# Dealing the rows of a mixture-of-experts layer to their places block by block, and turning each tile on VectorE

## The chip, the cores and the metric

The kernel runs on one core of one Trainium2 chip. The metric is device time in microseconds (us) for one execution. Three runs of the kernel before gave 1424.63, 1426.37 and 1427.61; their median, 1426.37, is the time that the change is measured against.

## What is computed

A GRU cell runs over 256 time steps for 8 sequences with state width 512. Its outputs, 2048 rows of 512 float32, go through a mixture of 8 experts, of which each row uses two, beside a shared expert that every row uses. The result is added to the input `x`.

```python
def cell(h, x):
    gi = x @ W_ih + b_ih
    gh = h @ W_hh + b_hh
    i_r, i_z, i_n = jnp.split(gi, 3, axis=-1)
    h_r, h_z, h_n = jnp.split(gh, 3, axis=-1)
    r = jax.nn.sigmoid(i_r + h_r)
    z = jax.nn.sigmoid(i_z + h_z)
    n = jnp.tanh(i_n + r * h_n)
    h_new = (1.0 - z) * n + z * h
    return (h_new, h_new)
...
probs = jax.nn.softmax(x @ w_gate, axis=-1)
topk_w, topk_ids = jax.lax.top_k(probs, 2)
topk_w = topk_w / jnp.sum(topk_w, axis=-1, keepdims=True)
combine = jnp.sum(topk_w[..., None] * jax.nn.one_hot(topk_ids, 8), axis=1)
act = _silu_and_mul(jnp.einsum('th,ehf->etf', x, w_gate_up))   # 512 -> 256
eo = jnp.einsum('eti,eih->eth', act, w_down)                   # 256 -> 512
routed = jnp.einsum('te,eth->th', combine, eo)
shared = _silu_and_mul(x @ w_sh_gate_up) @ w_sh_down           # 512 -> 1024 -> 512
return (routed + shared).reshape(orig_shape)
...
x = x + ffn(gru(cond_2048, x))
```

## The kernel before

**Stages.** Time is cut into 16 blocks of 16 steps, so a block holds 8 x 16 = 128 rows, one per partition. The profile shows four stages: loading and the first input projections (0 to 41.6 us), the recurrence (41.6 to 1154), a tail that finishes the last blocks' shared expert (1154 to 1204), and the tile stage, which does the routed experts (from 1204).

**The recurrence.** `step(n)` issues 32 small matmuls against the state and then a chain over VectorE (DVE) and ScalarE (ACT) to the new state. The schedule is written out by hand: between the matmuls of two steps TensorE (PE) gets a fixed amount of other work from `queue`: the input projections of the next block (`project`, line 331) and the shared expert of earlier blocks (line 785). In each step GpSimd (POOL) copies one column of `hn` to `last_hn` (line 523). That copy does no arithmetic that is needed; since POOL runs its instructions in order, it holds what stands behind it, such as the bias additions of `project` (line 425, `gi<-gi,bias`), until `hn` of that step is made.

**Routing.** After a block its rows are routed over the next block's steps: `choose`, `sum_logits`, `order_experts`, `weigh`, `count_places`, `give_places`. Then `enter` (line 637) writes for each row and each of its two experts one entry (row number and weight, 8 bytes) to a list `listed` in DRAM, at the row's place in its expert's part, by an indirect DMA of POOL; `send_rows` (lines 647 and 652) turns the block's states with one 128x512 transpose of DVE and stores the rows in token order to `rows` in DRAM. For block 0 `enter` runs eight times, once for each expert, in block 1. The last block's routing stands in the tail, in a hand-written list `routing` whose first numbers are places in the work of PE.

**The tail.** `lay_tiles` counts the rows of each expert, cuts each expert's part into tiles of 128 entries, reads the entries of all tiles back with one indirect DMA (line 697, `nT<-listed,at`), and makes `row` and `share`, the row numbers and weights of each tile, and `steer`, its expert. Meanwhile POOL loads the weights of two experts (line 170). SP, the engine that only issues DMAs, issues `send_rows`, then the stores of finished shared rows (`add_up`, line 824) and loads of `x` for the next ones (`load_again`, line 770).

**The tile stage.** 35 tiles are always run, with up to 4 more under a condition. `fetch_rows(i)` (line 836) gathers the tile's 128 rows from `rows` into `xr_i`, an indirect DMA of POOL; it is called two tiles ahead, and `xr` has three buffers. `before_` (lines 850 and 852) turns the rows: four 128x128 transposes on PE into PSUM, and one copy by ACT into `xrT`. The up matmuls (line 739), the activation (lines 726, 730, 731), the two transposes of the activation (line 750), the down matmuls (line 870) and the weighting by DVE into `y` (line 873) follow. At last an indirect DMA of POOL adds `y` to the rows of the output in DRAM (line 876). `y` has two buffers. `run_tile` lets three tiles overlap on PE:

```python
for work in [
    *(stages[0] if stages else []),     # before_ of tile i
    *ups[: NQ // 2],                    # first half of the up matmuls of tile i-1
    *(oldest[2] if oldest else []),     # the activation of tile i-2 is turned
    *ups[NQ // 2 :],
    *(oldest[3] if oldest else []),     # down matmuls of tile i-2
]:
```

**Waits between DMAs.** The framework tracks which DRAM tensor a DMA reads or writes, as a whole where the places come from an index. So each `enter` waits until the `enter` before it has landed, and each addition to the output waits for the one before it. The wait stands on the issuing engine, so everything behind it on POOL waits too.

Of the kernel before, what the change touches and what calls it, by code (L numbers as in the profile page):

```python
# [9 lines left out]
F32 = mybir.dt.float32  # L10
BF16 = mybir.dt.bfloat16
I32 = mybir.dt.int32
# [13 lines left out]
def kernel(  # L26
# [65 lines left out]
    NM = NTOK // P  # L92
    NW = NQ + NF
# [33 lines left out]
    def by_state(w):  # L127

        v = w.rearrange("(j q i) n -> j i q n", j=4, i=32)
        return [(slice(32 * j, 32 * j + 32), v[j]) for j in range(4)]  # L130

# [19 lines left out]
    h = state.tile([P, NQ, 32], F32, name="h")  # L151
# [34 lines left out]
    def load_up(e):  # L186
        for ps, src in by_state(w_gate_up[e]):
            load((we[ps, e, 0:NQ, :], src))
# [67 lines left out]
    first_place = counting("first_place", E, 0, NTOK, 0)  # L256
# [41 lines left out]
    listed = dram.tile([E * NM + 1, P, 2], F32, name="listed")  # L298
# [5 lines left out]
    load((listed[0 : E * NM], vacant), (listed[E * NM : E * NM + 1], vacant[0:1]))  # L304
# [229 lines left out]
    lg_of, rank_of, any_of, places_of, chosen, weight_of = {}, {}, {}, {}, {}, {}  # L534
    count = const.tile([P, E], BF16, name="count")
# [56 lines left out]
    def weigh_all(k):  # L592

        ch, w2 = chosen.pop(k), weight_of.pop(k)
        comb = said_0[:, :, 1]
        nc.vector.tensor_scalar(comb, ch[:, 0, :], w2[:, 0:1], None, ALU.mult)
        nc.vector.scalar_tensor_tensor(comb, ch[:, 1, :], w2[:, 1:2], comb, ALU.mult, ALU.add)
        nc.vector.tensor_scalar(
            said_0[:, :, 0], row_of.broadcast_to([P, E]), 0.0, None, ALU.add
        )  # L600
# [9 lines left out]
    def give_places(k):  # L610
        any_, ps = any_of.pop(k), places_of.pop(k)
        place = two.tile([P, E], F32, tag="place", name=f"place_{k}")
        nc.vector.tensor_tensor(place, ps, first_place, ALU.add)
        if k == 0:
            last = two.tile([P, E], F32, tag="last", name="last", bufs=1)
            nc.vector.tensor_scalar(last, any_, ahead, behind, ALU.mult, ALU.add)
            pl = two.tile([P, E], I32, tag="pl_0", name="pl_0", bufs=1)
            nc.vector.tensor_tensor(pl, place, last, ALU.add)
            nc.vector.tensor_copy(count, any_)
        else:  # L620
            ch, w2 = chosen.pop(k), weight_of.pop(k)
            nc.vector.tensor_tensor(ch, ch, place.unsqueeze(1).broadcast_to([P, 2, E]), ALU.mult)
            plf = two.tile([P, 2], F32, tag="plf", name=f"plf_{k}")
            nc.vector.tensor_reduce(plf, ch, AX.X, ALU.add)
            pl = two.tile([P, 2], I32, tag="pl", name=f"pl_{k}")
            nc.vector.tensor_copy(pl, plf)
            nc.vector.tensor_scalar(
                said[k % 2][:, :, 0], row_of.broadcast_to([P, 2]), float(k * TS), None, ALU.add
            )
            nc.vector.tensor_copy(said[k % 2][:, :, 1], w2)  # L630
            nc.vector.tensor_tensor(count, count, any_, ALU.add)
        places_of[k] = pl
# [11 lines left out]
    def send_rows(k):  # L644
# [6 lines left out]
        for j, c, ps in turns:  # L651
            nc.sync.dma_start(v[j, c, k * TS : (k + 1) * TS], hr[ps])

# [5 lines left out]
    def lay_tiles(part_no):  # L659

        if part_no == 0:
# [23 lines left out]
            spread = small([NT + 1], "spread", BF16)  # L685
            nc.vector.tensor_scalar(spread[:, 0:NT], ident[:, 0:NT], ex, None, ALU.mult)
            nc.vector.tensor_tensor(spread[:, NT:], ident[:, 0:1], cum[:, E - 1 : E], ALU.mult)
# [5 lines left out]
            nc.vector.scalar_tensor_tensor(no, ex, float(NM), no, ALU.mult, ALU.add)  # L693
            at = small([1], "at", I32)
            nc.vector.tensor_scalar(at, no, float(E * NM), None, ALU.min)
# [7 lines left out]
            laid.update(spread=spread, got=got)  # L703
        elif part_no == 1:
            ps = bank_of([P, NT + 1], "exp")[0]
            nc.tensor.matmul(ps, ones, laid["spread"], start=True, stop=True)
            steer = small([NT + 1], "steer", I32)
# [125 lines left out]
    def fetch_rows(i):  # L833
        if i < NT:
            xr_of[i] = xpool.tile([P, D], F32, tag="x", name=f"xr_{i}")
            nc.gpsimd.indirect_dma_start(
                out=xr_of[i],
                out_offset=None,
                in_=rows.rearrange("b t d -> (b t) d"),
                in_offset=bass.IndirectOffsetOnAxis(ap=laid["row"][:, i : i + 1], axis=0),  # L840
            )

    def tile_unit(i):
        box = {}

        def before_():
            ps = for_transposes([NQ, P], f"xrTp_{i}")
            xr = xr_of.pop(i)
            for q in range(NQ):
                nc.tensor.transpose(ps[:, q, :], xr[:, q * P : (q + 1) * P], ident)  # L850
            xrT = two.tile([P, NQ, P], F32, tag="xrT", name=f"xrT_{i}")
            nc.scalar.copy(xrT, ps)
# [104 lines left out]
    for k in range(NB):  # L957
# [7 lines left out]
        if k > 0:  # L965
# [5 lines left out]
            for t, (f, cost, busy) in enumerate(steps_):  # L971
                when(t + late, cost, busy, lambda f=f, k=k: f(k - 1))
            if k == 1:
                when(5, 0, 0.7, lambda k=k: weigh_all(k - 1))
# [48 lines left out]
    for e in (E - 4, E - 3):  # L1023
# [7 lines left out]
        (7 * MM, lambda k: lay_tiles(0)), (behind_them, lambda k: load_again(k - 1)),  # L1031
        (behind_them, load_again), (14 * MM, lambda k: lay_tiles(1)),
        (22 * MM, lambda k: lay_tiles(2)),
# [64 lines left out]
```

## Time and profile before

| | us |
|---|---|
| median of three runs | 1426.37 |
| the profiled execution, its own time | 1426.31 |
| its span (first to last instruction) | 1424.4 |
| loading and first projections | 0 to 41.6 |
| recurrence, block 0 and block 1 | 70.1 and 72.9 |
| recurrence, each of blocks 2 to 14 | 69.2 to 70.2 |
| tail | 1154 to 1204 |
| tile stage, first transpose to last instruction | 1204.0 to 1424.4 |
| PE busy in the tile stage up to 1412 | 204.0 of 208.0 |
| DVE, ACT and POOL busy in the same 208.0 | 56.7, 46.9 and 85.4 |

A line of a timeline reads: start and duration in us, engine, line of the kernel, operation, output<-inputs, shapes, count, and in brackets how long the engine stood idle before it and what ended that. "PEld" is PE loading weights, "SPq" a DMA issued by SP. The profiled execution lies 0.06 us from the median, and the span leaves 1.9 us of its time outside.

### The profile page before, as it was taken

To read this page: it belongs to the slowest core of one execution; us is meant where nothing else is said; L and a number is where in the kernel's file an instruction comes from. 1 tells how busy PE (TensorE), PEld (TensorE's weight loads), DVE (VectorE), ACT (ScalarE), POOL (GpSimd) and SP (SyncE) were. 2 spreads that over 40 slices of the span, in tenths; PEclk is the share of its full clock that TensorE was granted. 3 is DMA by queue.
4 is the path that set the end of the run, shared out by engine and by line. 5 is a ranking of instruction groups with operands and counts; after the bars stand their busy time and mean duration, and the time that the engine had idled before them with its cause. 6 is when DMAs were issued, how large, how long until landed. Compare 5 with 4: busy or idle time off the path is not lost.

```text
span 1424.4 us, 58403 instructions
## 1 busy us (share of the span) xinstructions
PE 1389.1 (98%) x24652; PEld 797.7 (56%) x24652; DVE 634.0 (45%) x2661; ACT 493.8 (35%) x2072; POOL 284.0 (20%) x525
## 2 busy tenths in 40 slices
PE   6999999999999999999999999999999999999995
PEld 2455557565666566656665666566656654444442
DVE  2345554455454545455544554554444541222221
ACT  0344343334333433343334343334343321222221
POOL 2233421212110201010101010101011221444442
PEclk9999999999999999999999999999999999999998
DMA  7233322122211111011111121111012444445543
GB/s 268 92 119 109 78 80 54 49 76 65 59 38 35 28 52 35 23 43 37 36 36 29 29 52 29 38 31 45 14 43 55 94 91 109 74 90 91 92 90 46
DMA packets 66885, 90.90 MB, mean 64 GB/s; under 512 B 12688, under 2 KB 44480, under 8 KB 66624
## 3 DMA queue, kind: packets, MB, share of 16 engines
q0 software_dynamic: 15104, 37.57, 12.5%
q1 hardware_dynamic: 50176, 48.60, 12.3%
q8 instruction: 195, 3.19, 1.0%
q10 hardware_dynamic: 1344, 1.00, 0.2%
q14 instruction: 66, 0.54, 0.1%
HBM read 56.80 MB, written 30.32 MB: 61 GB/s over the span
## 4 chain that ended last, share of the span: by engine, by line
PE 95%; DMA 2%; DVE 1%; ACT 1%; issue 1%; POOL 0%; SPq 0%; ACTq 0%; DVEq 0%; POOLq 0%
PE ps_rn L494 32%; PE gu_s L785 16%; PE ps_z L494 15%; PE gip L331 10%; PE gu_t L739 8%; PE po L331 8%; PE yp L870 4%; DMA gid_rz<-gi 1%; DMA x<-in_x_dram 0%; DMA we<-in_L_cond_b_hh_dram 0%; PE ps_x L850 0%; PE ps_rn L850 0%; PE ps_z L850 0%; DMA out_dram<-y,row 0%; PE lgp L542 0%
## 5 line engine op out<-in xcount | busy, mean ns | idle before, releaser
L494 PE MATMUL ps_rn<-we,hT 128*8 128x256 f32 x8192 | 492.9, 380 | 13.2 <-ACT ps_rn L466 8.9
L494 PEld LDWEIGHTS ps_rn<-we,hT 128*8 128x8 f32 x8192 | 224.3, 90 | 264.1 <-ACT ps_z L466 54.2
L494 PE MATMUL ps_z<-we,hT 128*8 128x128 f32 x8192 | 273.4, 273 | 0.0
L507 DVE STREAM_TRANSPOSE rT<-ps_rn 128x128 f32<-128x128 f32 x256 | 81.1, 317 | 431.1 <-PE ps_rn L494 431.1
L494 PEld LDWEIGHTS ps_z<-we,hT 128*8 128x8 f32 x8192 | 228.1, 90 | 51.3 <-issue 0.5
L511 ACT ACTIVATE rT<-rT 128x32 f32<-128x32 f32 x256 | 58.5, 229 | 529.5 <-DVE rT L507 522.1
L523 POOL COPY last_hn<-hn 128x1 f32<-128x1 f32 x256 | 46.8, 183 | 885.4 <-DVE hn L522 878.6
L785 PE MATMUL gu_s<-hc,wsu 128*32 128x256 f32 x3072 | 188.6, 379 | 0.8 <-ACT gi L424 0.8
L331 PE MATMUL gip<-we,xT 128*32 128x512 f32 (+3 forms) x1872 | 186.9, 522 | 1.6 <-DVE xT L224 1.6
L785 PEld LDWEIGHTS gu_s<-hc,wsu 128*32 128x32 f32 x3072 | 102.5, 110 | 58.9 <-issue 10.8
L739 PE MATMUL gu_t<-we,xrT 128*128 x280 | 131.7, 593 | 0.3 <-issue 0.3
L331 PE MATMUL po<-wsd,act_s 128*32 128x512 f32 (+3 forms) x1272 | 130.1, 509 | 0.0
L331 PEld LDWEIGHTS gip<-we,xT 128*32 128x32 f32 x1872 | 60.1, 111 | 71.3 <-issue 58.8
L507 DVE STREAM_TRANSPOSE zT<-ps_z 128x128 f32<-128x128 f32 x256 | 79.0, 309 | 0.4 <-PE ps_z L494 0.4
L528 ACT COPY hc<-hT 128x32 f32<-128x32 f32 x192 | 47.4, 247 | 91.3 <-DVE hT L525 90.0
L876 POOL DMA_INDIRECT out_dram<-y,row x35 | 55.5, 1585 | 112.9 <-DVE y L873 102.5
L730 DVE TENSOR_TENSOR act_t<-gu_t,act_t 128x256 f32<-128x256 f32 x35 | 14.9, 425 | 131.4 <-ACT act_t L726 131.4
L466 ACT COPY ps_rn<-seeds_n 128x128 f32<-128x128 f32 x256 | 69.0, 270 | 8.8 <-DMA seeds_n<-gid_n 0.6
L507 DVE STREAM_TRANSPOSE nT<-ps_rn 128x128 f32<-128x128 f32 x256 | 70.2, 274 | 0.0
L514 DVE TENSOR_TENSOR rT<-nT,rT 128x32 f32<-128x32 f32 x256 | 51.2, 200 | 41.3 <-ACT rT L511 40.7
L466 ACT COPY ps_rn<-seeds 128x128 f32<-128x128 f32 x256 | 68.9, 269 | 1.5 <-DVE rT L514 0.6
L739 PEld LDWEIGHTS gu_t<-we,xrT 128*128 128x128 f32 x280 | 47.9, 190 | 34.9 <-issue 34.7
(168 smaller groups left out, 1221.6 us busy)
## 6 DMA issues: line engine op xcount, KB each, us to landing
we<-in_L_ffn_w_gate_up_dram POOLq DMA_DIRECT2D x32, 256.0 KB, 3.8
seeds<-gid_rz SPq DMA_DIRECT2D x252, 32.0 KB
gid_rz<-gi SPq DMA_DIRECT2D x15, 512.0 KB
wsu<-_L_ffn_w_sh_gate_up_dram POOLq DMA_DIRECT2D x16, 256.0 KB, 3.8
rows<-hr SPq DMA_DIRECT2D x128, 32.0 KB
we<-in_L_ffn_w_down_dram POOLq DMA_DIRECT2D x16, 256.0 KB, 4.7
again<-in_x_dram SPq DMA_DIRECT2D x16, 256.0 KB
out_dram<-again SPq DMA_DIRECT2D x16, 256.0 KB
```

The costliest lines, as they stand in the source:

```text
L331: nc.tensor.matmul(ps[32 * c : 32 * c + 32], lhs(c), rhs, start=start, stop=stop, skip_group_check=True,)
L466: nc.scalar.copy(gate_of[g], src)
L494: nc.tensor.matmul(banks[g][32 * j : 32 * j + B, 0 : n_ * P].rearrange("b (a k i) -> b a k i", a=n_, k=NQ), hT[:, q, 0:B], whh_v[:, q, j, ...
L507: nc.vector.transpose(gT.rearrange("p a b -> p (a b)"), gate_of[g])
L511: nc.scalar.activation(r, r, AF.Sigmoid)
L514: nc.vector.tensor_tensor(r, nT[:, :, 0:B], r, ALU.mult)
L523: nc.gpsimd.tensor_copy(last_hn, hn[:, 0, 0:1])
L528: nc.scalar.copy(hc_of_block(k).rearrange("p g q (c t) -> p q g c t", t=TS)[:, :, :, :, t], new.rearrange("p q (g c) -> p q g c", c=2),)
L739: nc.tensor.matmul(box["ps"], lhs(q), w_up(q), start=(q == 0), stop=(q == NQ - 1))
L785: nc.tensor.matmul(box["ps"][32 * g : 32 * g + 32, two_i, :], wsu[c][:, q, two_i, fs], hc_of[m][:, :, q, :], start=(two_i == 0 and q == 0) ...
L870: nc.tensor.matmul(box["y"], lhs, rhs, start=(f == 0), stop=(f == NF - 1))
L876: nc.gpsimd.indirect_dma_start(out=out.rearrange("b t d -> (b t) d"), out_offset=bass.IndirectOffsetOnAxis(ap=laid["row"][:, i : i + 1], a ...
```

## The change

The rows no longer lie in token order for the tiles to gather. After `send_rows` a block's 128 rows are read back to SBUF in token order (`read_rows`, an SP DMA), and two indirect DMAs of POOL (`deal_rows`), one for each of a row's experts, scatter them to a second DRAM tensor, `dealt`, where each expert has 17 blocks of 128 places. In the tail eight more indirect DMAs write rows of zeros behind the last row of each expert, so that a tile's unused places hold zeros; a last block of `dealt` is all zeros from the start. A tile is then 128 rows that lie together. `fetch_rows` reads the tile's number from `steer` into a register of SP and issues four plain DMAs, each to 32 partitions: partition 32j+t gets elements 128j to 128j+127 of rows t, 32+t, 64+t and 96+t. One transpose of DVE in 32x32 blocks makes `xrT` of it; the four transposes of PE and the copy of ACT are gone. Since the features of a row now lie on the partitions in another order, an expert's up weights are loaded in plain blocks of 128 rows and not by quarters.

```diff
-    def by_state(w):
-
-        v = w.rearrange("(j q i) n -> j i q n", j=4, i=32)
-        return [(slice(32 * j, 32 * j + 32), v[j]) for j in range(4)]
...
-    h = state.tile([P, NQ, 32], F32, name="h")
+    h = we[:, 0, 3, 0:P].rearrange("p (q i) -> p q i", q=NQ)
...
     def load_up(e):
-        for ps, src in by_state(w_gate_up[e]):
-            load((we[ps, e, 0:NQ, :], src))
+        for q in range(NQ):
+            load((we[:, e, q, :], w_gate_up[e, q * P : (q + 1) * P, :]))
...
+    dealt = dram.tile([E * NR + 1, P, D], F32, name="dealt")
...
+    nothing = we[:, 1, 2]
+    nc.gpsimd.memset(nothing, 0.0)
...
+    load((dealt[E * NR], nothing))
...
+    def read_rows(k):
+
+        rows_of[k] = two.tile([P, D], F32, tag="y", name=f"rb_{k}")
+        nc.sync.dma_start(rows_of[k], rows[:, k * TS : (k + 1) * TS, :])
+
+    def deal(tile_, at):
+        nc.gpsimd.indirect_dma_start(
+            out=dealt.rearrange("r p d -> (r p) d"),
+            out_offset=bass.IndirectOffsetOnAxis(ap=at, axis=0),
+            in_=tile_,
+            in_offset=None,
+        )
+
+    def deal_rows(k, i):
+        deal(rows_of[k], rows_at[k][:, i : i + 1])
...
         elif part_no == 1:
-            ps = bank_of([P, NT + 1], "exp")[0]
+            ends = small([E], "ends")
+            nc.vector.scalar_tensor_tensor(
+                ends, laid["cnt"], part, first_place, ALU.add, ALU.add
+            )
+            ends_i = small([E], "ends_i", I32)
+            nc.vector.tensor_copy(ends_i, ends)
+            zeros = gi.rearrange("p j g n -> p (j g n)")[:, 0:D]
+            nc.gpsimd.memset(zeros, 0.0)
+            for e in range(E):
+                deal(zeros, ends_i[:, e : e + 1])
+        elif part_no == 2:
+            ps = bank_of([P, 2 * NT + 1], "exp")[0]
...
     def fetch_rows(i):
         if i < NT:
-            xr_of[i] = xpool.tile([P, D], F32, tag="x", name=f"xr_{i}")
-            nc.gpsimd.indirect_dma_start(
-                out=xr_of[i],
-                out_offset=None,
-                in_=rows.rearrange("b t d -> (b t) d"),
-                in_offset=bass.IndirectOffsetOnAxis(ap=laid["row"][:, i : i + 1], axis=0),
-            )
+            xr_of[i] = xpool.tile([P, NG, P], F32, tag="x", name=f"xr_{i}")
+            at = nc.values_load(
+                laid["steer"][0:1, NT + 1 + i : NT + 2 + i],
+                engines=(mybir.EngineType.SP,),
+                min_val=0,
+                max_val=E * NR,
+            )
+            src = dealt[bass.ds(at, 1)].rearrange("o (g t) (j m) -> j t (o g) m", g=NG, j=4)
+            for j in range(4):
+                nc.sync.dma_start(xr_of[i][32 * j : 32 * j + 32], src[j])
...
         def before_():
-            ps = for_transposes([NQ, P], f"xrTp_{i}")
-            xr = xr_of.pop(i)
-            for q in range(NQ):
-                nc.tensor.transpose(ps[:, q, :], xr[:, q * P : (q + 1) * P], ident)
             xrT = two.tile([P, NQ, P], F32, tag="xrT", name=f"xrT_{i}")
-            nc.scalar.copy(xrT, ps)
+            nc.vector.transpose(
+                xrT.rearrange("p q t -> p (q t)"),
+                xr_of.pop(i).rearrange("p g (q i) -> p q g i", q=NQ),
+            )
...
+            when(9, 0, 0, lambda k=k: read_rows(k - 1))
+            for i in range(2):
+                when(12 + i, 0, 0, lambda k=k, i=i: deal_rows(k - 1, i))
...
-        (7 * MM, lambda k: lay_tiles(0)), (behind_them, lambda k: load_again(k - 1)),
-        (behind_them, load_again), (14 * MM, lambda k: lay_tiles(1)),
-        (22 * MM, lambda k: lay_tiles(2)),
+        (7 * MM, lambda k: lay_tiles(0)), (8 * MM, lambda k: lay_tiles(1)), (9 * MM, read_rows),
+        (11 * MM, lambda k: deal_rows(k, 0)), (11 * MM, lambda k: deal_rows(k, 1)), (behind_them, lambda k: load_again(k - 1)),
+        (behind_them, load_again), (14 * MM, lambda k: lay_tiles(2)),
+        (22 * MM, lambda k: lay_tiles(3)),
         (22 * MM, lambda k: fetch_rows(0)), (22 * MM, lambda k: fetch_rows(1)),
```

In the built program of the changed kernel every one of the eight zero deals and of the two deals of the last block waits for the completion of the deal before it, and the first DMA of `fetch_rows(0)` waits for the last of them. On POOL the tail's order is: the two `enter`, two loads of weights, the read of the list, one load of weights, the zeros, the eight zero deals, three loads, the two deals of the last block, one load.

## The prediction

> **What bounds the kernel now.** I read the page's engine shares and chain first, then the tile stage's timeline, where the removed work stands, then POOL and PE in the tail, and last the end of the chain.
>
> ```profile
> PE 1389.1 (98%) x24652; PEld 797.7 (56%) x24652; DVE 634.0 (45%) x2661; ACT 493.8 (35%) x2072; POOL 284.0 (20%) x525
> ...
> PE 95%; DMA 2%; DVE 1%; ACT 1%; issue 1%; POOL 0%; SPq 0%; ACTq 0%; DVEq 0%; POOLq 0%
> ```
>
> PE is busy for 98% of the span and carries 95% of the chain that ends last, so an instruction taken from PE is worth its own time, until something else ends later. One tile, from the timeline of the tile stage:
>
> ```profile
> 1233.33 1.57 POOL L876 DMA_INDIRECT out_dram<-y,row  x1 [2.93 <-DVE y L873]
> ...
> 1237.90 0.60 PE L850 MATMUL ps_x<-ident,xr 128*128 128x128 f32 x4
> ...
> 1238.34 1.88 PE L739 MATMUL gu_t<-we,xrT 128*128 x4
> ...
> 1239.14 1.58 POOL L876 DMA_INDIRECT out_dram<-y,row  x1 [2.95 <-DVE y L873]
> ```
>
> A tile takes 5.81 us (1233.33 to 1239.14). The four transposes hold PE from 1237.90 to 1238.34, 0.44 us. POOL's additions wait for DVE here, that is for PE.
>
> POOL in the tail, and PE where the tail becomes the tile stage:
>
> ```profile
> 1163.44 1.04 POOL L637 DMA_INDIRECT listed<-said,pl  x1 [6.21 <-DVE count L631]
> 1166.85 1.01 POOL L637 DMA_INDIRECT listed<-said,pl  x1 [2.37 <-DMA listed<-said,pl]
> 1167.86 0.59 POOL L170 DMA_DIRECT2D we<-in_L_ffn_w_down_dram  x1
> 1168.43 0.60 POOL L170 DMA_DIRECT2D we<-in_L_ffn_w_gate_up_dram  x1
> 1172.23 1.02 POOL L697 DMA_INDIRECT nT<-listed,at  x1 [3.20 <-DMA listed<-said,pl]
> ...
> 1184.61 1.00 POOL L836 DMA_INDIRECT xr<-rows,row  x1 [8.55 <-DVE share L718]
> ```
>
> ```profile
> 1203.97 0.65 PE L850 MATMUL ps_x<-ident,xr 128*128 128x128 f32 x4
> ...
> 1205.35 3.67 PE L739 MATMUL gu_t<-we,xrT 128*128 x8 [0.28 <-issue]
> ```
>
> PE has shared work until 1203.97. The first gather leaves at 1184.61, so the tile stage's first rows have some 15 us of cover. An indirect DMA that waits for the one before it starts 3.41 us (1163.44 to 1166.85) to 5.38 us (1166.85 to 1172.23) after it.
>
> The end of the chain shows the same for the additions:
>
> ```profile
> 1407.30 4.65 DMA out_dram<-y,row
> ...
> 1412.70 1.55 POOL out_dram L876
> ```
>
> The addition issued at 1407.30 lands after 4.65, and the next starts at 1412.70: a link of 5.40 us, 4.65 to land and 0.75 for POOL to wake and issue.
>
> **The change, part by part.**
>
> *The tile stage.* Without the four transposes PE needs 5.81 - 0.44 = 5.37 us per tile. DVE's 128x512 transpose is priced by the one of `send_rows` (L647, 0.71 us). DVE has 56.7 us busy in 208.0 and takes 35 x 0.71 = 24.9 more; it is off the path, since the turn of tile i is wanted only one tile later. ACT loses its copies, PE waits for neither. POOL loses 35 gathers of 0.98 us. But the additions form a chain of their own:
>
> ```profile
> xr<-rows,row POOLq DMA_INDIRECT x35, 4.1
> out_dram<-y,row POOLq DMA_INDIRECT x35, 4.7
> ```
>
> These are the median times from issue to landing. With 4.7 + 0.75 a link is 5.45 us. Before, that was under PE's 5.81; it is over the new 5.37, so the additions, not PE, pace the new stage. Bounds: 5.37 (PE) and 5.73 (1379.31 to 1385.04, the one place in the stage where POOL waited for an addition). I take 5.45, the median. Before, the first up matmul stood at 1205.35 and the last addition at 1412.70: 207.35. After: 10.55 (1205.35 to the first addition at 1215.90) less one tile's 0.44, and 34 x 5.45 = 185.3: 195.4. **-11.9 us** (-14.7 with PE alone, -2.4 with 5.73).
>
> SP gets four plain DMAs and a register load per tile. Eight stores of 512-byte pieces took SP 5.55 us in `send_rows`, 0.69 each, so 2.8 per tile; the register load would have to cost over 2.6 before SP paces the stage. I take it as hidden, two tiles ahead; the cover gone, each tile would be late by the excess.
>
> A page of the Trainium skill prices the removed work otherwise: "VectorE: DVE Perf Modes", The three transpose paths, gives a 128x128 transpose 390 ns on TensorE, which would make an estimated 35 x 4 x 0.39 = 55 us of gain. Those are bfloat16 and single; in this trace four float32 ones, back to back, take 0.44 us, and the sum goes by that.
>
> *The tail.* This is new on the path. The read of the list ends on POOL at 1173.25; one load follows (0.56), then 128x512 zeros, which I estimate at 0.5 from the 0.20 of a 128x128 memset of POOL and 0.10 of a tiny one. So the first zero deal starts at 1174.4. Ten deals, each waiting for the one before, make nine links and a landing. No row shows a plain scatter of 2 KB rows. Below stands `enter`, the same write of 8-byte rows: 3.41. Above stands the addition, which reads as well: 5.40. Nearest is the gather, the same bytes in as many rows with no addition: 3.6 for the one at 1187.19, 4.1 in the median, plus 0.75: 4.35 to 4.85. I take 4.5, of which 3.75 to land: 1174.4 + 9 x 4.5 + 3.75 = 1218.6. The loads of weights lie in the same queue, one ahead of the first deal and three ahead of the ninth; the second `enter` of the tail, with loads in its way, took 2.0 more than the first, and I add 2.8 for both places (0 to 5): 1221.5.
>
> Then SP wakes (0.3), issues four DMAs (3 x 0.69 to the last), which land after 2.58 (the `seeds` load on the chain at 29.05): 1226.4. DVE turns the rows in 0.71, with its wake 0.8: the first up matmul stands at 1227.2, not 1205.35. **+21.9 us**, for which PE is idle from 1204. Bounds: 1213.5 (+8.1) with links of 3.41 and no loads in the way, 1238.4 (+33.1) with 5.40 and 5. Three things stand behind the waits: SP's last two stores, needed ten us later by the first addition; four loads of the sixth expert, not needed for half of the tile stage; the next `fetch_rows`, which follow in 3 us each while an up stage takes 3.44.
>
> The Trainium skill's "DMA: Bandwidth & Descriptors", Anatomy of one DMA, speaks against a chain of dependent writes in kind but prices it lower: about 2.0 us fixed plus bytes at 436 GB/s. By that a deal of 256 KB lands in an estimated 2.6 us, and with the same 0.75 the chain is ended some 11 us earlier and the change about even. The landings above are all over 2.6, so the rows decide.
>
> *The recurrence.* Each block gains an SP read and two deals on POOL at steps 12 and 13. SP's wait for `send_rows`, issued two or three steps earlier, is over by then, and the loads queued behind it (`seeds`) are wanted four steps later. POOL waits in the second deal for the first, less than two steps, and behind it stands only `last_hn`, wanted by the next `hn`. From block 2 on no bias addition stands near the deals in the built order: nothing. Block 1 differs, with eight `enter` and bias additions among them:
>
> ```profile
> 146.25 1.28 POOL L425 TENSOR_TENSOR gi<-gi,bias 128x512 f32<-128x512 f32 x1
> 146.27 1.32 DVE L515 TENSOR_TENSOR rT<-nT,rT 128x32 f32<-128x32 f32 x1
> ```
>
> POOL had waited for an `enter`, the bias addition slid into DVE's chain, and a 0.19 us operation of DVE took 1.32; that step took 6.24 us where its neighbours take 4.3. Block 1 is 3.5 over the others for this. Two deals more at its steps 12 and 13, just ahead of a bias addition, cost one such step more: **+2.0 us** (0 to 5).
>
> The rest is small: plain weight loads in place of quarters (256 KB each as before), a dozen tiny DVE operations, a memset of 0.5 us at the start.
>
> **Sum.** -11.9 + 21.9 + 2.0 = +12.0 on the profiled execution's 1426.31, 0.06 under the median: **1438.3 us**.
>
> **The rivals.**
>
> *The cover nearly holds* (faster). If a scattered write of 2 KB rows lands like `enter`'s, the tile stage starts at 1213.5, and with PE pacing it and no loss in block 1 the sum is 8.1 - 14.7 = -6.6: 1419.7. For it: the two `enter` at 1163.44. Against: an `enter` moves 1 KB, a deal 256 KB, and the gather, which moves as much, lands later. With my other terms kept, the links must fall under 3.3 for no change; with every other term at its best, under 4.05.
>
> *The tile stage gains nothing as well* (much slower). If the additions are slowed by the plain loads beside them to 5.73, or SP paces the stage at about that, it gains 2.4: 21.9 + 2.0 - 2.4 = +21.5, 1447.8. For it: DMA is busy 47% of that stage. Against: half of the indirect DMAs there are the gathers, which go.
>
> *It balances.* Links near 3.5: +2, 1428. That the deals don't wait, so that the change would do only what it removes, is excluded by the built program, where each of them waits for the last.
>
> **How the numbers follow.** Forecast 0.74, much slower 0.12, faster 0.08, balance 0.06. 0.2% is 2.9 us, about what a measurement of this kernel can tell. Only the third is under 1423.5, only the fourth within: faster 0.08, same 0.06, slower 0.86. The range leaves out most of the faster case and the far end of the slow one: 1426 to 1453.
>
> **What would show it.** Right: PE idle for over 15 us after 1204, ended by DVE's turn of `xr`; on POOL eight deals, 4 to 5 us apart, each waiting for a deal; additions 5.4 to 5.5 us apart, now waiting for a DMA. Wrong in size: links under 3.5 or over 5.4. Wrong in kind: the first `fetch_rows` before 1200, or tiles paced by SP.

## The result, and the profile after

The changed kernel takes 1431.94 us in the median (1424.12 to 1440.62, 22 runs), the kernel before beside it 1426.24 (1424.63 to 1429.48, 22 runs): a ratio of 1.0034, 95% interval 1.0023 to 1.0045, or +5.7 us where +12.0 was forecast. Measured twice more, on two chips, the ratio was 1.0073 (1.0056 to 1.0090) and 1.0075 (1.0059 to 1.0090), some +10.5 us. In the first measurement the changed kernel's 22 times lie 16.5 us apart and those of the kernel before 4.9; in the two others 6 times of the changed kernel lie 7 apart, 17 of the kernel before 7 to 8. That the ratio differs from one measurement to the next belongs to the explanation. The profiled execution took 1429.51, its span is 1427.7.

The page's engine line of the chain that ended last (shares of the span) gives PE 90% where it had 95%, and DMAs, issue and POOL the rest:

```profile
PE 90%; DMA 4%; issue 2%; DVE 1%; POOL 1%; ACT 1%; SPq 0%; POOLq 0%; ACTq 0%; DVEq 0%
```

The tail, from the timelines of POOL and PE (start, duration, engine and line, operation, idle time before it and what ended that):

```profile
1178.17 1.03 POOL L661 DMA_INDIRECT dealt<-gi,ends_i  x1 [0.28 <-POOL gi L731]
1184.08 0.98 POOL L661 DMA_INDIRECT dealt<-gi,ends_i  x1 [4.88 <-DMA dealt<-gi,ends_i]
...
1201.65 0.96 POOL L661 DMA_INDIRECT dealt<-gi,ends_i  x1 [2.02 <-DMA dealt<-gi,ends_i]
...
1212.84 0.99 POOL L661 DMA_INDIRECT dealt<-rb,pl  x1 [2.38 <-DMA dealt<-rb,pl]
```

```profile
1202.04 5.33 PE L331 MATMUL po<-wsd,act_s 128*32 128x512 f32 x48
...
1220.12 6.84 PE L769 MATMUL gu_t<-we,xrT 128*128 x12 [12.75 <-DMA xr<-dealt]
```

The ten deals stand in a row, each waiting for the one before, and PE stands idle for 12.75 us until the first rows have been fetched. That is the mechanism of the prediction, with shorter links: 2.98 us (1198.67 to 1201.65) for the shortest, 5.91 for the first, 34.67 for all nine. The chain that ended last shows what a short link is made of (start, duration, what):

```profile
1198.67 2.71 DMA dealt<-gi,ends_i
1201.38 0.27 issue
```

The deal lands after 2.71, and POOL starts the next one 0.27 later.

The additions, from the costliest groups (busy, mean ns of one, then POOL's idle time before them and what ended most of it) and from the DMA issues (the last number is the median from issue to landing):

```profile
L908 POOL DMA_INDIRECT out_dram<-y,row x35 | 54.3, 1552 | 151.0 <-DMA out_dram<-y,row 93.2
```

```profile
out_dram<-y,row POOLq DMA_INDIRECT x35, 4.7
```

POOL's waits ahead of an addition are now ended for the most part by the addition before (93.2 of 151.0 us), not by DVE. The 34 links take 186.5, 5.485 each.

Term by term, for two pairs of profiled executions, the second pair (runs e13 and e12 below) from one chip. Each difference is taken between the same two marks of the kernel before and after (last state: the last `last_hn`; then the first up matmul, the last addition's start, the end of the span):

| | forecast | first pair | second pair |
|---|---|---|---|
| up to the last state | +2.0 | 1153.91 to 1157.23: +3.3 | 1155.45 to 1153.68: -1.8 |
| last state to first up matmul | +21.9 | 51.44 to 62.89: +11.5 | 51.42 to 63.74: +12.3 |
| first up matmul to last addition | -11.9 | 207.35 to 198.06: -9.3 | 207.46 to 208.45: +1.0 |
| last addition to the end | 0 | 11.70 to 9.52: -2.2 | 11.87 to 9.73: -2.1 |
| span | +12.0 | +3.3 | +9.4 |

So the tail's term was nearly twice too large in both pairs, and the gain of the tile stage is there in one execution and gone in another. The second pair comes near the forecast because the two errors cancel, not because its terms were right.

### The profile page after: what moved, and what is told of

Same layout as the page of the kernel before. It is cut to its first block, busy times and chain, and to the rows that moved or that the text cites. A ratio compares the mean times of both kernels' runs of the same rounds, so it can differ in the third digit from the quotient of the medians.

```text
span 1427.7 us, 58770 instructions
## 1 busy us (share of the span) xinstructions
PE 1375.5 (96%) x24512; PEld 787.6 (55%) x24512; DVE 658.3 (46%) x2703; ACT 473.1 (33%) x2037; POOL 288.9 (20%) x533
## 3 DMA queue, kind: packets, MB, share of 16 engines
q8 instruction: 194, 3.18, 0.9%
## 4 chain that ended last, share of the span: by engine, by line
PE 90%; DMA 4%; issue 2%; DVE 1%; POOL 1%; ACT 1%; SPq 0%; POOLq 0%; ACTq 0%; DVEq 0%
PE ps_rn L494 32%; PE ps_z L494 15%; PE gu_s L815 14%; PE gip L331 10%; PE gu_t L769 9%; PE po L331 6%; PE yp L902 4%; DMA dealt<-gi,ends_i 1%; DMA out_dram<-y,row 1%; DMA gid_rz<-gi 1%; DMA x<-in_x_dram 0%; DMA listed<-said,pl 0%; DMA we<-in_L_cond_b_hh_dram 0%; DVE rT L514 0%; DMA seeds<-gid_rz 0%
## 5 line engine op out<-in xcount | busy, mean ns | idle before, releaser
L769 PE MATMUL gu_t<-we,xrT 128*128 x280 | 132.9, 598 | 12.8 <-DMA xr<-dealt 12.8
L769 PEld LDWEIGHTS gu_t<-we,xrT 128*128 128x128 f32 x280 | 51.1, 193 | 64.7 <-issue 57.0
L908 POOL DMA_INDIRECT out_dram<-y,row x35 | 54.3, 1552 | 151.0 <-DMA out_dram<-y,row 93.2
L522 DVE TENSOR_TENSOR hn<-hT,rT 128x32 f32<-128x32 f32 x256 | 49.3, 193 | 38.7 <-ACT rT L517 11.4
```

The source lines that it names most:

```text
L522: nc.vector.tensor_tensor(hn, hT[:, :, 0:B], nn, ALU.subtract)
L769: nc.tensor.matmul(box["ps"], lhs(q), w_up(q), start=(q == 0), stop=(q == NQ - 1))
L908: nc.gpsimd.indirect_dma_start(out=out.rearrange("b t d -> (b t) d"), out_offset=bass.IndirectOffsetOnAxis(ap=laid["row"][:, i : i + 1], a ...
```

## The experiments

The theory had two parts: the serial deals in the tail cost some 12 us of PE's idle time, and the tile stage without transposes is paced by the chain of additions, whose landing is not the same in every execution. The rivals: that the idle stretch comes from SP's plain fetches or from loads of weights; that bytes, not links, set the deals' length; that fetches or PE pace the stage. Where nothing else is said, an experiment is an edit of the changed kernel. Their readings, from the same marks (e5 is left out, see there; e3 and e13 are single executions):

| | last state to first up matmul | PE idle | us per tile (34 links) | ratio to before (95%) |
|---|---|---|---|---|
| before; again (e13) | 51.4; 51.4 | 0.3; 0.3 | 5.79; 5.79 | 1 |
| changed; again (e7, e12) | 62.9; 64.4, 63.7 | 12.8; 14.2, 13.6 | 5.49; 5.87, 5.77 | 1.0034; 1.0073, 1.0075 |
| e1, three zero deals | 54.2 | 3.2 | 5.81 | 1.0022 (1.0011 to 1.0033) |
| e5b, zeros in block 15 | 52.3 | 1.8 | 5.78 | 1.0006 (0.9995 to 1.0017) |
| e3, zeros twice | 85.9 | 35.7 | 5.51 | 1455.55 us, one run |
| e15, loads behind | 67.8 | 17.6 | 5.75 | 1.0065 (1.0044 to 1.0085) |
| e2, plain writes | 65.4 | 15.2 | 5.31 | 0.9986 (0.9974 to 0.9997) |
| e8, e5b with plain writes | 52.3 | 1.8 | 5.31 | 0.9892 (0.9877 to 0.9908) |
| e9, whole rows | 64.6 | 14.5 | 5.73 | 1.0077 (1.0056 to 1.0099) |
| e11, three fetches | 65.3 | 15.2 | 5.66 | 1.0055 (1.0042 to 1.0068) |
| e4, block 0's deals late | 64.8 | 14.7 | 5.75 | 1.0091 (1.0071 to 1.0110) |
| e14, zeros brought by SP | 52.2 | 1.8 | 5.89 | 1.0014 (1.0001 to 1.0027) |

**e1: fewer deals.**

```diff
-            for e in range(E):
-                deal(zeros, ends_i[:, e : e + 1])
+            deal(zeros[:, 0:D], near)          # 16 rows behind each expert's last
+            for i in range(2):                 # 128 x 4 rows, groups of four
+                nc.gpsimd.indirect_dma_start(
+                    out=dealt.rearrange("r (g s) d -> (r g) (s d)", s=4), ...
```

> The eight zero deals of the tail are replaced by three: one that writes 16 rows behind each expert's last, and two of 128 rows of 8 KB. Ten deals in a chain become five. Theory (the number of serial links sets the start of the tile stage, 3.85 a link): the wide deals land later than the narrow ones, about 6.5 a link, so the chain shortens by 9 x 3.85 - (2 x 3.85 + 2 x 6.5) = 14 at most; the idle stretch of PE of 12.75 shrinks to 0 to 3 and the time lies at 1415 to 1421, under the kernel before. Rival (bytes, not links: the two wide deals move 1 MB each against 256 KB, so the chain's 2.56 MB become 2.75 MB): the chain keeps its length within 2 us, and so does the time, 1430 to 1434.

The two wide deals made links of 6.47 and 8.47 (in the second, three loads of weights are issued behind that deal's landing), and the last of the five deals was issued 10 to 11 us sooner after the last state than the last of the ten. PE's idle stretch fell to 3.24, close to the 0 to 3 of the theory. The time did not follow: 1430.52, where the forecast was under the kernel before. The tile stage took 5.81 a tile, no less than before the change (5.79), so that nothing is left of its gain. What the edit is worth depends on the measurement of the changed kernel that it is held against: some 7 us by the ratios of 1.0073 and 1.0075, nothing clear of noise by 1.0034. It comes near the kernel before and no further.

**e5 and e5b: no zeros in the tail.** Both deal 256 rows of zeros for each expert in block 15 of the recurrence, behind the counts after block 14; the last block's rows then overwrite some of them.

```diff
+            if k == NB - 1:
+                for i, t in enumerate((9, 10, 11, 14, 15)):
+                    when(t, 0, 0, lambda i=i: deal_zeros(i))
...
-        (7 * MM, lambda k: lay_tiles(0)), (8 * MM, lambda k: lay_tiles(1)), (9 * MM, read_rows),
+        (7 * MM, lambda k: lay_tiles(0)), (9 * MM, read_rows),
```

> The zeros are written in block 15 of the recurrence, behind the counts that hold after block 14, by five deals (one of 128 rows of 2 KB, four of 128 rows of 8 KB, 256 rows for each expert); the tail keeps only the last block's two deals, and a POOL memset of 128x2048 is made at the start. Theory (the changed kernel loses its gain in the tail, because the chain of ten deals ends 12.75 us after PE has run out of shared work): the last deal lands some 30 us earlier, PE goes from the shared expert to the tile stage without an idle stretch, as before the change, and the tile stage and its end keep their -9.3 and -2.2: the span is 1427.7 - 12.8 - about 1.5 of low clock behind it = 1413 to 1416, ratio to the kernel before 0.991 to 0.995. Rival A (the idle stretch comes from the plain fetch by SP or from the wait of the register load, not from the deals): first up matmul still 10 us or more behind the end of the shared work, time about 1431. Rival B (the tile stage is slower as such once it starts early, since DMAs of weights lie beside it): idle stretch gone, but the stage takes 203 or more in place of 198, time 1420 or more.

In e5 I had put the source of zeros where the recurrence's weights `whh` lie. It ran 39 tiles in place of 35, 1451.4 us, and nothing rests on it. e5b keeps the zeros in the last expert's place, whose weights then load later:

> The zeros are written in block 15 by five deals as before, from space that is free then (the last expert's weights are loaded later for it); the tail keeps the last block's two deals. Two theories of what limits the changed kernel. Both say that PE's idle stretch goes (0 to 2 us) and that the first up matmul stands at about 1206. If the tile stage is paced by the additions at 5.6 to 5.8, it is no shorter than before the change, and the time is 1206 + 11.5 + 34 x 5.7 + 9.5 + 1.9 = 1423, ratio to the kernel before 0.995 to 0.999. If it is paced by PE or by a steady 5.485, the time is 1415, ratio 0.991. The rival that POOL's or SP's loads, not the zeros, hold the first fetch: first up matmul still at 1215 or later, time 1431 or more.

```profile
1207.22 5.33 PE L348 MATMUL po<-wsd,act_s 128*32 128x512 f32 x48
...
1214.36 5.39 PE L818 MATMUL gu_t<-we,xrT 128*128 x12 [1.81 <-issue]
```

The first up matmul follows the last shared matmuls after 1.81: the zero deals, and neither SP's fetches nor the loads, made the idle stretch. The recurrence ended 8 later here than in e12 (start 1.4, block 1 3.6 and block 15 3.0 longer), so the stage starts only 3 earlier; and it takes 5.78 a tile. The time is 1431.36: 10.6 under the changed kernel of the same call (1441.95), and no different from the kernel before, since the tile stage with its additions is no shorter than before the change.

**e2: additions become writes.**

```diff
-                    compute_op=ALU.add,
```

> A tile's result is written to the output's rows instead of being added to them (so the sums are left out); everything else is as in the changed kernel, and each write still waits for the one before. Theory (the additions pace the tile stage at 5.485 a tile, over PE's 5.37, since each lands after 4.7): a write without reading lands after 3.2 to 3.7, the link falls to about 4.3, POOL waits for DVE again, and PE paces the stage at 5.37: 34 x 0.115 = 3.9 us less, 1428, and the times scatter less. Rival (PE and its weight loads pace the stage at 5.485 and POOL's waits for the DMA are only what is left over): no change, 1430 to 1433.

The same lines of POOL's timeline, a tile apart:

```profile
1305.72 0.96 POOL L908 DMA_INDIRECT out_dram<-y,row  x1 [4.41 <-DVE y L905]
1311.09 0.96 POOL L908 DMA_INDIRECT out_dram<-y,row  x1 [4.41 <-DVE y L905]
```

POOL waits for DVE again, all steady tiles take 5.37 (PE's pace as forecast), the write lands after 3.0 in place of 4.7 to 4.9, and the 12 times lie 5.2 apart. The expected 1428 became 1425.62. So what the adding costs beyond a plain write stands between the changed tile stage and PE's pace.

**e8: both at once** (e5b and e2 together).

> Zeros in block 15 and, besides, a tile's result written in place of added (the sums are left out). Theory (two costs, each by itself: the deals in the tail cost some 12, the additions the difference from 5.37 a tile): first up matmul at about 1206, 5.37 a tile: 1206 + 12.3 + 34 x 5.31 + 11.7 + 1.9 = 1412, ratio 0.988 to 0.991. Rival (DMAs of weights or the fetches limit the stage once it starts early): over 5.45 a tile, 1416 or more.

1415.7 us, 14.6 under the kernel before (1430.28 beside it). Neither edit alone does this: e5b comes to 1.0006 of the kernel before, e2 to 0.9986, both together to 0.9892. In the profiled execution (1418.25, the slowest of the five) the first up matmul to the last write takes 190.8 where e13 has 207.5. Of these 16.7 the last link, 3.43 in place of PE's 5.37, is 1.9; the rest, 14.8, is what the prediction gave the stage with PE alone (-14.7). That the whole time also comes to -14.6 is partly chance: in the profile the recurrence ended 6.6 later than in e13.

**e7, e13 and e12: the same kernels again.**

> The changed kernel itself once more, beside the next ones. Theory (its tile stage is paced by additions whose landing differs from execution to execution, 4.7 to 5.0, since the runs with additions showed 5.485, 5.745 and 5.81 a tile and the one with plain writes 5.37): 5.6 to 5.8 a tile here, idle stretch of PE ahead of the first tile 12 to 15, median 1435 to 1441, and executions 10 or more apart. Rival (the slow tile stages of the two other kernels were due to their own edits): 5.45 to 5.5 a tile and a median of 1430 to 1434.

> The kernel before itself once more, for its profile beside the changed kernel's in one call. Theory (PE's 5.81 a tile hides the additions before the change): additions land after 4.7 to 5.0 as in the other runs, POOL's waits for them are few, and the tile stage keeps 5.81 a tile and some 207 from the first up matmul to the last addition. Rival (this chip or moment slows every tile stage): 5.85 or more a tile here too.

> The changed kernel beside the kernel before. Theory (the additions' landing is what differs between executions, and only the changed kernel feels it): over 5.5 a tile, first addition to last 187 to 200, idle stretch 12 to 15, 1433 to 1442, ratio 1.003 to 1.009. Rival (the first profile's 5.485 is the rule): 1431 to 1433, 5.45 to 5.5 a tile.

The kernel before kept 5.79 a tile, though its additions landed after 4.9 on that chip, as the changed kernel's did; the changed kernel took 5.87 and 5.77, where e7's expectation had 5.6 to 5.8. (The additions of the first profile landed after 4.7 in the median, those of e7 and e12 after 4.9.) The groups of e13 and of e12:

```profile
L876 POOL DMA_INDIRECT out_dram<-y,row x35 | 55.5, 1586 | 112.9 <-DVE y L873 105.4
```

```profile
L908 POOL DMA_INDIRECT out_dram<-y,row x35 | 54.3, 1552 | 161.3 <-DMA out_dram<-y,row 96.5
```

DVE's timeline in e12 shows how the additions take over:

```profile
1340.29 0.42 DVE L760 TENSOR_TENSOR act_t<-gu_t,act_t 128x256 f32<-128x256 f32 x1 [2.70 <-ACT act_t L756]
...
1341.92 0.75 DVE L905 TENSOR_SCALAR y<-yp,share 128x512 f32<-128x512 f32 x1 [0.75 <-DMA out_dram<-y,row]
...
1347.58 0.75 DVE L905 TENSOR_SCALAR y<-yp,share 128x512 f32<-128x512 f32 x1 [1.03 <-DMA out_dram<-y,row]
...
1351.04 0.42 DVE L760 TENSOR_TENSOR act_t<-gu_t,act_t 128x256 f32<-128x256 f32 x1 [2.09 <-ACT act_t L756]
...
1359.80 0.75 DVE L905 TENSOR_SCALAR y<-yp,share 128x512 f32<-128x512 f32 x1 [2.50 <-DMA out_dram<-y,row]
```

The activation keeps PE's 5.37 a tile (1340.29 to 1351.04 is two tiles), while `y` waits longer each time for one of its two buffers, which an addition that has not landed still reads. When that lag is used up, DVE's next operation, the turn of `xr`, comes late and PE waits for it (0.40 to 0.81 at each of the tiles 30 to 33). In the first profile DVE waited once for an addition (3.6 us), here 13 times (42.4).

**e9 and e11: what lengthens the additions.** e9 leaves bytes and count of the fetches, but takes whole rows; e11 has no fetch after the third tile.

```diff
-            src = dealt[bass.ds(at, 1)].rearrange("o (g t) (j m) -> j t (o g) m", g=NG, j=4)
+            src = dealt[bass.ds(at, 1)].rearrange("o p (g m) -> (o p) g m", g=NG)     # e9
...
+            if i > 2:
+                xr_of[i] = kept[i % 3]                                             # e11
+                return
```

> Each fetch of 32 partitions takes 32 whole rows of 2 KB instead of 128 pieces of 512 bytes (so a tile's elements come to the wrong places); bytes and number of DMAs are the same. Theory A (the 512-byte pieces crowd the engines that carry the additions, and so lengthen their landing): additions land 0.2 to 0.4 earlier, 5.37 to 5.45 a tile, time 5 to 10 under the changed kernel of the same call. Theory B (an addition's own reading and writing sets its landing, whatever lies beside it): the pace stays within 0.1 of that kernel's, and the time within 3.

> Only the first three tiles are fetched; all later tiles compute on those rows again (so the routed part is not the reference's); the additions and all else stay. Theory A (the fetches' transfers lie beside the additions and lengthen their landing): additions land after 4.3 to 4.65 and the stage falls to PE's 5.37 or close to it, 10 or more under the changed kernel of the same call. Theory B (an addition that reads and writes 128 rows of 2 KB takes what it takes): the pace stays within 0.1 a tile of the changed kernel's, the time within 3.

The mean links of tiles 1 to 14, 15 to 28 and 29 to 33 are 5.59, 6.01 and 5.62 in e12, 5.60, 5.89 and 5.65 in e9, 5.63, 5.70 and 5.63 in e11. By the time theory B held for both: e9's median, 1441.69, lies 0.3 under that of the changed kernel of its call (e7), e11's, 1435.88, lies 2.6 under e12's. The pace a tile fell by 0.14 and 0.10, a little more than B allowed and far from the 5.37 to 5.45 that theory A asked for. So the size of the pieces shows no clear effect, and without the fetches a link is still 5.6 to 5.7: most of it is the addition's own. Whether the fetches add the 0.3 in the middle of the stage is not shown, since two profiles of the same kernel differ there by more: 5.47 in the first, 6.21 in e7. Why the middle tiles suffer, and why the first profile (5.52, 5.47, 5.49) did not, stays open.

**e15 and e3: the links of the tail.** e15 holds all loads of weights back until the last block's deals are issued; e3 makes each zero deal twice.

```diff
-        if loads:
-            loads.popleft()()
+        for _ in range(2):
+            if loads and len(routing) <= 6:
+                loads.popleft()()
...
-            for e in range(E):
-                deal(zeros, ends_i[:, e : e + 1])
+            for e in range(2 * E):
+                deal(zeros, ends_i[:, e // 2 : e // 2 + 1])
```

> In the tail all loads of weights by POOL stand behind the last block's deals; nothing else changes. In the changed kernel the first two links of the chain of deals took 5.5 to 6.5, the undisturbed ones 2.97. Theory (the loads of weights that are under way lengthen the first links): all links near 3.0 to 3.5, the nine together 27 to 31 in place of 34.7 to 35.8, the first up matmul 4 to 8 nearer to the last state, time 3 to 8 under the changed kernel if the loads do no harm later. Rival (the first deals are slow because of the stores of SP, or by themselves): the first two links stay over 5, the chain within 2 of 35.

> Every zero deal is made twice, 16 in place of 8. Theory (the chain of deals is serial and it alone sets the start of the tile stage): the first up matmul moves by 8 links of 2.97 to 3.6 = 24 to 29, the time by the same. Rival (part of the 12 to 15 of PE's idle stretch is something else that runs beside the deals): less than 20.

e3's first up matmul on PE, and two of its later deals on POOL:

```profile
1243.54 8.16 PE L769 MATMUL gu_t<-we,xrT 128*128 x12 [35.74 <-DMA xr<-dealt]
```

```profile
1214.86 0.96 POOL L661 DMA_INDIRECT dealt<-gi,ends_i  x1 [2.02 <-DMA dealt<-gi,ends_i]
1217.84 0.96 POOL L661 DMA_INDIRECT dealt<-gi,ends_i  x1 [2.02 <-DMA dealt<-gi,ends_i]
```

Eight links more put the first up matmul 23.0 later (62.9 to 85.9, against the first profile), where 8 x 2.98 is 23.8: nothing hides a link. The time of this one execution, 1455.55, is 14 to 24 over the three medians of the changed kernel; its additions were of the faster kind (5.51 a tile). In e15 the first two links were 4.61 and 4.91, where the first profile, e7 and e12 have 5.9 to 6.5 and 3.5 to 5.6, and the nine together 31.9 in place of 34.7 to 35.8, between what the theory and the rival named: the loads are a part of what disturbs the first links; the rest was not taken apart. And e15 was not faster, for a reason that nobody had stated:

```profile
1219.06 0.71 DVE L881 STREAM_TRANSPOSE xrT<-xr 128x512 f32<-128x512 f32 x1 [12.45 <-DMA xr<-dealt]
...
1223.48 1.19 PE L769 MATMUL gu_t<-we,xrT 128*128 x1 [17.64 <-DMA we<-in_L_ffn_w_down_dram]
```

The rows were turned by 1219.77, but PE waited till 1223.48 for a load of weights, the last of which was issued at 1215.63. That load is one of down weights, which no up matmul reads: since the expert's number comes from a register, the first up matmul waits for all loads into `we`, not for its own expert's.

**e4 and e14: the recurrence.** e4 makes block 0's deals in block 2. e14 is e5b with zeros brought by SP and without the copies to `last_hn` from step 8 of block 15.

```diff
+                if k == 2:
+                    when(2 + i, 0, 0, lambda i=i: deal_rows(0, i))            # e4
...
+        if n < (NB - 1) * TS + 8 or n == T - 1:                               # e14
             nc.gpsimd.tensor_copy(last_hn, hn[:, 0, 0:1])
```

> Block 0's two deals are made in steps 2 and 3 of block 2 instead of steps 12 and 13 of block 1. Theory (deals that stand among the eight entries and the bias additions of block 1 push a bias addition into DVE's chain, 1.8 us in one step; the step of 5.98 with its low clock is another matter): block 1 falls from 76.7 to 74 to 75, block 2 stays at 69.2 to 70.2, time -2 against the changed kernel: 1429 to 1430. Rival (block 1 is longer because its loads stand one place later in the queue, through the load of the zero block ahead of them): block 1 stays at 76 to 77 and the time at 1432.

> As the version with zeros in block 15, with two edits to that block: the source of zeros comes by four DMAs of SP from DRAM in place of four memsets of DVE, and the copies to last_hn are left out from the block's step 8 on, so that a deal that waits on POOL does not hold the next hn. Theory (block 15's 72.6 in place of 69.4 came from these two): block 15 back at 69.2 to 70, time 3 under the former version, ratio to the kernel before 0.996 to 0.999. Rival (the wide writes themselves slow PE's or DVE's work of that block): block 15 stays over 72, ratio 1.000 to 1.002.

e4: block 1 took 71.3, but the time was 1439.77 (1.0091, 1.0071 to 1.0110): no gain over the changed kernel's 1.0073 and 1.0075. Block 1 took 72.5 and 72.1 in e7 and e12 against 72.9 and 73.7 in the kernel before, so there is no steady loss to undo; over the twelve profiles with this block 1 it scatters from 72.0 to 78.1. e14: block 15 was back at 69.7, as its theory said, and the first up matmul stood at 1209.19, 5.2 sooner than in e5b, of which 1.0 was there at the start of the recurrence. But its tile stage took 5.89 a tile, and the time is 1430.41, ratio 1.0014 (1.0001 to 1.0027), where 0.996 to 0.999 was expected. No version with additions beats the kernel before: the first up matmul can be put some 12 nearer to the last state, which takes away the loss, but with additions at 5.78 to 5.89 a tile the stage brings no gain.

## Why the prediction was right or wrong

**What bounds, and the direction: right.** Slower, by a chain of serial deals on which PE waits, with the tile stage handed from PE to the additions. PE's pace without transposes is 5.37 as worked out (e2, e8), and the tile stage that starts on time and is paced by PE is worth the -14.7 of the bounds (e8: -16.7, of which -1.9 is its last link).

**The tail, +21.9: the mechanism right, the size wrong.** This is the step that failed: the price of a link, 4.5, with 2.8 for the loads on top. Measured are +11.5 and +12.3, and PE's idle stretch was 12.75 to 14.2 and not over 15. By parts, in the first profile: nine links of 3.85 and not 4.5 (-5.8); the 2.8 for the loads is already in the first link, 5.91, and was counted on top of a median that also held disturbed DMAs (-2.8); the last landing 2.75 and not 3.75 (-1.0); SP's fetch from that landing to DVE's turn 3.5 and not 4.9 (-1.4: an issue of SP took 0.32 in the median, not 0.69); the turn with its wake 1.0 and not 0.8 (+0.2). The zeros began 0.4 later than I put them, after allowing for the later end of the recurrence.

I made a link of the gather's landing, as the nearest row of the same bytes, and of the 0.75 that POOL took to wake and issue an addition. For seven of the nine links the first profile has the landing: 2.71 to 5.63, 3.70 in the mean, so that the 3.75 was near it. But POOL started the next deal 0.27 after the landing in six of the seven and 0.77 in one: the wake is most of what was wrong with a link. A deal with nothing beside it needs 2.98, of which 2.71 is the landing; the gather's 4.1 is a median in a stage in which additions lie beside it.

The Trainium skill's "DMA: Bandwidth & Descriptors", Anatomy of one DMA, whose fixed 2.0 us and bytes at 436 GB/s would make an estimated 2.6 of such a landing, was set aside because the landings shown were longer (all but the 2.58 of the `seeds` load). It was close to an undisturbed deal, 2.71. The page's fit is for one DMA; the rows held the company of others besides.

**The tile stage, -11.9: right in the first profile within 2.6, wrong as a constant.** I took the link of the median, 5.45. It was 5.49, 5.87 and 5.77 in three executions. The bound of 5.73 was named, but as a rival with a chance of 0.12, and only as part of a much slower case; in the second pair it happened (+1.0), alone. Before the change only links that PE did not cover could show what an addition takes, and the two that ended on one, 5.73 and the last, 5.40, lie on both sides of the first profile's mean: a median could not stand for all executions. Another 1.5 us of loss, ahead of the first addition, is PE's clock (below).

**The end, not priced: -2.2.** From the last addition's start to the end of the span both changed executions need 2.2 less than before. No run takes this apart.

**The recurrence, +2.0: not shown.** +3.3 and -1.8 up to the last state. In block 1 of the first profile the step with the second deal, an entry and the bias addition took 6.11 for 5.11, as described; another 1.7 of that block were the clock's. In e7 and e12 the block was no longer than before.

**Beside the sum: one wrong reason.** That "four loads of the sixth expert" are "not needed for half of the tile stage" was wrong: the first up matmul waits for them all (e15). It cost nothing in the first profile, where the last load, issued at 1213.84, landed after 3.0, before the rows came.

**The rivals.** "Cover nearly holds" needed links under 4.05 with every other term at its best. The links came to 3.85, but the other terms did not follow. "It balances" asked for links near 3.5 and named 1428; on links it was the nearest, on the first median it was 3.9 off.

## What to carry to other kernels

Price a link of a serial chain of DMAs by what it does undisturbed and add its neighbours where they lie, instead of a median from a busy stage; to add them to such a median counts them twice. Take the engine's wake from the same kind of DMA as the landing: here it was 0.27 behind a deal and 0.75 behind an addition. When work is taken off the engine that paces a loop, look for the next chain and for how steady it is: a chain of DMAs with links of 5.4 to 5.9 us is nearly hidden under 5.81 and shows every slow landing once the cover is 5.37, so that the kernel's time follows the landings from one measurement to the next. An earlier start of such a loop is worth its own time (e5b: 10.6) and no more: the loop stays as long as its longest chain.

## What was not expected of the hardware

PE's granted clock fell behind short waits. The first profile's stretches after the idle time of the tail (window and its length, busy time of PE, PEld, DVE, ACT and POOL, then PE's granted clock, the DMA share and GB/s):

```profile
1207.00:1220.00 13.00, 0.37 (x4) 0.00 (x0) 1.67 (x3) 0.00 (x0) 3.75 (x6) 0.59 0.50 169
1220.00:1224.00 4.00, 3.88 (x6) 1.87 (x7) 0.71 (x1) 0.00 (x0) 0.00 (x0) 0.62 0.45 117
```

The first twelve up matmuls took 6.84 there and 7.55 to 8.36 after idle stretches of 13.6 to 15.2 (e2, e7, e12); they took 5.39 after 1.8 or 3.24 (e5b, e1). In block 1 a shorter wait sufficed. PE's timeline in the first profile, and then in e9:

```profile
147.83 3.59 PE L494 MATMUL ps_rn<-we,hT 128*8 128x256 f32 x32 [2.07 <-DVE hT L525]
...
153.84 1.90 PE L494 MATMUL ps_rn<-we,hT 128*8 128x256 f32 x32
```

```profile
160.18 3.18 PE L494 MATMUL ps_rn<-we,hT 128*8 128x256 f32 x32 [2.04 <-DVE hT L525]
```

The 32 matmuls that take 1.91 took 3.59 and 3.18, at a granted clock of 0.51 from 147.8 to 151.3 in the first. These are the two profiles with the longest block 1 (76.7 and 78.1). A wait of two microseconds cost them 1.7 and 1.3 more than itself.

Why 2.04 and 2.07 were enough and e1's 3.24 were not is a matter of where the waits lie. In every trace here the changes of the clock lie whole multiples of 3.41 us apart, as on a grid, whatever the program does (half clock from 147.86 to 151.27 and from 1209.41 to 1223.06 in the first profile: one step and four). Two neighbouring steps of that grid in the first profile, and two in e1 (columns as above):

```profile
144.45:147.86 3.41, 1.34 (x23) 0.34 (x16) 2.92 (x6) 0.76 (x4) 2.25 (x4) 1.00 0.45 120
147.86:151.27 3.41, 3.41 (x36) 1.31 (x40) 1.10 (x1) 0.10 (x1) 1.55 (x2) 0.50 0.28 68
```

```profile
1202.63:1206.05 3.42, 1.95 (x20) 0.39 (x12) 1.38 (x2) 0.00 (x0) 0.00 (x0) 1.00 0.36 111
1206.05:1209.46 3.41, 1.65 (x4) 0.87 (x5) 0.71 (x1) 0.00 (x0) 0.00 (x0) 1.00 0.36 99
```

The 2.07 lie in one step (PE busy 1.34 of 3.41), and the clock is halved for the next. The 3.24 are split over two steps, 1.47 and 1.76, and the clock stays at 1.00 in the step after them too. In all 16 kept traces, from the start of the recurrence on, each of the 28 steps at full clock with 2.04 us or more of PE idle time was followed by one at half clock, and none with 1.80 or less was.

The Trainium skill's "TensorE: Matmul & The Clock Gate", The HAM clock gate, gives a window of about 3.4 us that runs free of the program, and the grid agrees with it. It lets the clock fall after an idle window of that length; here 2.04 us of idle time within one window were enough.
